# Batch norm and last layer of a graph network: PSUM operands, two GpSimd buffers, another division into parts, and h one stage ahead

## The chip, the core and the metric

The kernel runs on one core of a Trainium2 chip. The metric is the device time of one execution in microseconds. These engines and queues matter: TensorE (PE, with its weight loads as PEld), VectorE (DVE), ScalarE (ACT), GpSimd (POOL), and the DMA queue that SyncE (SP) issues. [...]

## The reference, cut to what matters

There are 128 graphs of 128 nodes and 64 features, and four layers, each of which adds to `x`. The change touches the end of layer 2 (a batch norm over all graphs) and layer 3.

```python
# layer 2: y has been computed and scaled to unit rows
m = mask[..., None]; cnt = jnp.sum(mask)
mean = jnp.sum(y * m, axis=(0, 1)) / cnt
var = jnp.sum((y - mean) ** 2 * m, axis=(0, 1)) / cnt
y = ((y - mean) / jnp.sqrt(var + BN_EPS) * gamma + beta) * m
x = x + jax.nn.relu(y)
# layer 3
h = jnp.maximum(_layernorm(x, axis=-1), 0.0)
messages = jnp.einsum('bij,bjh->bih', adjacency, h)
node_in = jnp.concatenate([h, messages], axis=-1)
x = x + jnp.tanh(node_in @ W1 + b1) @ W2 + b2
```

The mean and variance of layer 2 need every graph, so nothing of layer 3 can begin before layer 2's `y` of the last graph is known.

## The kernel before, in words

The work is tiled into 32 groups of 4 graphs; a tile of a group is 128 nodes by 4x64 values, all in float32. Layers 0, 1 and 2 of the groups run in one long pipeline that takes most of the span. `layer2_norm` (line 645) of a group leaves `y` in SBUF (`ys[g]`), and `add_sums` (line 670) adds its weighted sum to `ysum` in PSUM by TensorE. When the last group has come through, lines 771 to 776 have subtracted a shift from every `y`, squared it on ScalarE and added it to `ysq`. `total` (line 675) picks the wanted blocks of such a sum with VectorE (`own`) and adds them up with products by ones. Lines 779 to 789 make from both totals the two rows of the batch norm, `factor` and `summand` (together `affine_all`).

Then the end begins. The 32 groups are divided into parts (`PARTS`, line 52). For each group of a part `normed` (line 803) does these steps:

- L806 and L807 multiply by the factor and add the summand, in place in `ys[g]`. VectorE does this for the first part, GpSimd for all others.
- L808 multiplies by the node mask, which lies in PSUM (`nm_ps`), on VectorE.
- L809 takes the maximum with 0 and adds it to `x`, on VectorE.
- L811 takes the statistics of layer 3's layer norm, one instruction for each of the 4 graphs, on VectorE.

After the last group of a part `roots` (line 813) turns the part's statistics into `rstd3` and `less3`, with five or six small steps of VectorE, a square root on ScalarE (L823) and a reciprocal (L824). [...] between this square root and layer 3's tanh it loads a table (`ACT_TABLE_LOAD`).

Layer 3 of a group has three stages. `layer3_gather` (line 831) loads the transposed adjacency by DMA, computes `h`, multiplies `h` by the identity and by the adjacency on TensorE (16 products into `ps_hm`) and copies the result to SBUF on ScalarE (`hm`, L848). For groups below `LATE` (18) `h` is made by four activations on ScalarE (L841); from 18 on by two steps of VectorE (L836 and L307), and GpSimd adds the last bias to `x` (L838). `layer3_tanh` multiplies by W1 and takes the tanh on ScalarE (L855). `layer3_end` multiplies by W2, adds to `x` on VectorE (L863, `o`) and stores the result by DMA. The loop at lines 875 to 888 calls, for each group g of a part, a share of `normed` for the next part, then gather of g, tanh of g-1 and end of g-2.

That is the order in which the program states its steps. Within it a scheduler of the language may move a step forward on its engine where its inputs are there, so the engines' own orders differ somewhat: VectorE was up to ten groups ahead with `normed`. The language also sets all semaphores, from which steps read and write which tiles.

[...] Three pairs of banks are the tiles `blks`; the last pair, `fixed`, holds `nm_ps` at the end, and the other four banks with two more go round as `end_bank`.

Of the kernel before, what the change touches and what calls it, by code (L numbers as in the profile page):

```python
# [9 lines left out]
F32 = mybir.dt.float32  # L10
# [4 lines left out]
ALU = mybir.AluOpType  # L15
# [3 lines left out]
P = 128  # L19
F = 64  # L20
G = 4
NP = G // 2
H0 = 192
LN_EPS = 1e-5
BN_EPS = 1e-5

# [20 lines left out]
FIRST, FIRST_R = 0, ORDER.index((None, FULL))  # L47
N_PREPARE, N_AFTER = 14, 26
PACE, LAG = 0.85, 2.5
LATE = 18  # L50
LASTS = 1.9
PARTS = [2, 4, 6, 6, 6, 8]
AHEAD = 3
NBLK = 3
W = NP * H0
# [18 lines left out]
def network(ctx, tc, io, out, over=None, x1=None):  # L74
# [203 lines left out]
    def over_f(ap):  # L278

        return ap.unsqueeze(2).to_broadcast([P, G, F])  # L280

    def over_g(ap):

        return ap.unsqueeze(1).to_broadcast([P, G, F])

    def bank(name):
        return ps.tile([P, 512], F32, tag="ps", name=name)

    def flat(t):
        return t.rearrange("p a n -> p (a n)")  # L290
# [354 lines left out]
    def layer2_norm(g):  # L645
        xt, adjT, y = xs[g], adjTs[g], ys[g]
        h = yield from layernorm_relu(xt)
        zT = gathered(h, adjT, "zT")
        yield
        py = biased("L2_gnn_bias", F)  # L650
        project_pairs(py, zT, wbn, F)
        pyf = py[:, 0 : G * F]
        yf = y.rearrange("p b f -> p (b f)")
        nc.scalar.copy(yf, pyf)
        sq = work.tile([P, G, F], F32, tag="sq", name="sqy")
        nc.scalar.activation(sq.rearrange("p b f -> p (b f)"), pyf, AF.Square)
# [18 lines left out]
    def total(sums, name):  # L675
# [3 lines left out]
        pt = bank(name)  # L679
        for b in range(G):  # L680
            matmul(pt[:, 0:F], ones[0:G, :], own[:, b, :], start=b == 0, stop=b == G - 1)
        return pt[:, 0:F]


    rcnt = keep.tile([P, 2], F32, name="rcnt")
# [74 lines left out]


    spare = iter(range(10 ** 6))
    fixed = blks[NBLK - 1]

    def end_bank(name):

# [15 lines left out]
    nc.vector.scalar_tensor_tensor(moved[:, 0, :], total(ysum, "ps_row"), rcnt[:, 0:1], shift, ALU.mult, ALU.subtract)  # L782
    nc.vector.tensor_tensor(moved[:, 1, :], moved[:, 0, :], moved[:, 0, :], ALU.mult)
    nc.vector.scalar_tensor_tensor(factor, total(ysq, "ps_sq"), rcnt[:, 0:1], moved[:, 1, :], ALU.mult, ALU.subtract)
# [10 lines left out]
    rstd3 = keep.tile([P, NG, G], F32, name="rstd3")  # L795
    less3 = keep.tile([P, NG, G], F32, name="less3")
    NS = 6

    def part_stats(gs):
        t = work.tile([P, G, F], F32, tag="sqv", name="stats")  # L800
        return flat(t)[:, 0 : len(gs) * G * NS].rearrange("p (g b s) -> p g b s", b=G, s=NS)

    def normed(g, stats, engine):

        xt, y = xs[g], ys[g]
        engine.tensor_tensor(y, y, over_g(affine_all[:, 0, :]), ALU.mult)  # L806
        engine.tensor_tensor(y, y, over_g(affine_all[:, 1, :]), ALU.add)  # L807
        nc.vector.tensor_tensor(y, y, over_f(nm_ps[:, g * G : (g + 1) * G]), ALU.mult)  # L808
        nc.vector.scalar_tensor_tensor(xt, y, 0.0, xt, ALU.max, ALU.add)  # L809
        for b in range(G):  # L810
            nc.vector.bn_stats(stats[:, b, :], xt[:, b, :])  # L811

    def roots(gs, stats):
        r, less = rstd3[:, gs[0] : gs[-1] + 1, :], less3[:, gs[0] : gs[-1] + 1, :]
# [5 lines left out]
        nc.vector.tensor_tensor(r, s0, s1, ALU.add)  # L820
        late = gs[0] >= LATE
        nc.vector.tensor_tensor(less if late else s1, stats[:, :, :, 1], stats[:, :, :, 4], ALU.add)
        nc.scalar.activation(r, r, AF.Sqrt, bias=eps, scale=1.0 / F)  # L823
        nc.vector.reciprocal(r, r)  # L824
        if not late:
            nc.vector.scalar_tensor_tensor(less, s1, -0.5, r, ALU.mult, ALU.mult)


    hms, tTs = {}, {}

    def layer3_gather(g):
        adjT = adjp.tile([P, G, P], F32, tag="adjT", name="adjT")
        nc.sync.dma_start(flat(adjT), saved[g])
        h = work.tile([P, G, F], F32, tag="h", name="h")
        if g >= LATE:
            nc.vector.scalar_tensor_tensor(ys[g], over_f(less3[:, g, :]), -0.5, xs[g], ALU.mult, ALU.add)  # L836
            relu_scaled(ys[g], rstd3[:, g, :], h=h)
# [30 lines left out]
        parts.append(range(at, at + n))  # L868
        at += n
    assert at == NG  # L870
    stats = part_stats(parts[0])
    for g in parts[0]:
        normed(g, stats[:, g], nc.vector)
    roots(parts[0], stats)
    for gs, nxt in zip(parts, parts[1:] + [[]]):

        stats, done = part_stats(nxt) if nxt else None, 0
# [11 lines left out]
    layer3_tanh(NG - 1)  # L889
    layer3_end(NG - 2)  # L890
    layer3_end(NG - 1)

    if over is None:
        return
# [155 lines left out]
```

## Time and profile before

| what | us |
|---|---|
| median of 3 runs | 1395.79 |
| lowest and highest | 1392.44, 1399.84 |
| the profiled execution | 1398.05 |
| its span in the profile | 1396.2 |
| last group's sums begin on TensorE | 1268.81 |
| first `h` begins | 1287.08 |
| last square root of `roots` | 1355.57 |
| last gather begins | 1384.69 |
| GpSimd's last L807 ends | 1321.0 |

Times within the span count from its start. Over the whole span TensorE is busy 88%, VectorE 84%, ScalarE 71% and GpSimd 19% of the time. A row of a group of instructions gives the line, the engine, the operation, what it writes and reads, the shapes, how many there were, their busy time and mean length in ns, and the engine's idle time before them. Because a later instruction may start while the one before it ends, the distance between two starts can be less than a length. A helper's line stands for all of its callers: every product has line 103, so products are told apart by the tiles.

### The profile page before, as it was taken

Reading aid. Unit: us, or ns where it says so; the run is one execution under the profiler, and the core shown is the slowest. Engines: PE = TensorE matmul, PEld = TensorE weight load, DVE = VectorE, ACT = ScalarE, POOL = GpSimd, SP = SyncE. Lnnn points to the kernel's source line nnn. Section 1 sums busy time; section 2 is a strip of 40 time slices with the busy share of each in tenths; the row PEclk is TensorE's granted clock in tenths of the full one; section 3 lists DMA queues with packets and bytes.
Section 4 is the critical chain, followed back from the end, with each engine's and each line's share of the span. In section 5 each row is a group of like instructions: output and inputs, shape, how many; then the busy total and the mean of one; then the engine's idle time right before and its main releaser. Section 6 shows DMA issues by size and latency. Waiting matters only on the chain.

```text
span 1396.2 us, 29319 instructions
## 1 busy us (share of the span) xinstructions
PE 1232.2 (88%) x10964; PEld 959.3 (69%) x10964; DVE 1167.8 (84%) x2629; ACT 990.8 (71%) x1883; POOL 270.6 (19%) x322
## 2 busy tenths in 40 slices
PE   3788999999999999999999999999999999995787
PEld 1467777777777777777777777776777777763566
DVE  6898888888888888888888888888898888866973
ACT  1677777777777777777777777777777777753783
POOL 3111111111111111111111111111111111015830
PEclk9899999999999999999999999999999999997889
DMA  5443222322323222222222222223222212200345
GB/s 120 131 120 98 67 66 78 83 83 84 83 76 83 84 75 75 76 63 75 66 78 84 83 84 83 75 83 84 76 75 79 62 59 60 76 9 15 93 112 126
DMA packets 108788, 110.97 MB, mean 79 GB/s; under 512 B 42895, under 2 KB 88220, under 8 KB 108636
## 3 DMA queue, kind: packets, MB, share of 16 engines
q1 hardware_dynamic: 108636, 109.00, 28.5%
q8 instruction: 89, 1.46, 0.5%
q14 instruction: 63, 0.52, 0.1%
HBM read 52.70 MB, written 35.29 MB: 63 GB/s over the span
## 4 chain that ended last, share of the span: by engine, by line
PE 65%; ACT 17%; DVE 13%; issue 2%; SPq 1%; DMA 1%; DVEq 0%; POOL 0%; ACTq 0%; POOLq 0%
PE blk L103 24%; PE ps_pr L103 10%; ACT blk L560 9%; DVE acc L583 6%; PE ps_ag L103 5%; PE ps_p L103 5%; PE ps_sA L103 5%; PE ps_o L103 3%; PE ps_sB L103 3%; PE ps_q L103 2%; PE ps_ah L103 2%; PE ps_hm L103 2%; ACT q L465 2%; DVE leftT L424 1%; PE ps_key L103 1%
## 5 line engine op out<-in xcount | busy, mean ns | idle before, releaser
L583 DVE SCALAR_TENSOR_TENSOR acc<-blk,acc 128x768 f32<-128x768 f32 x576 | 543.1, 950 | 65.0 <-PE blk L103 38.9
L560 ACT COPY blk<-psort 128x768 f32<-128x768 f32 x544 | 436.1, 806 | 134.1 <-DVE acc L583 132.2
L103 PE MATMUL blk<-q,oh 128*128 128x192 bf16 x3072 | 318.2, 246 | 34.5 <-ACT blk L560 34.3
L103 PEld LDWEIGHTS <-oh 128*128 128x128 bf16 x3072 | 259.1, 98 | 89.3 <-issue 84.3
L103 PE MATMUL blk<-near_q,ohn 128*128 128x192 bf16 x1536 | 199.7, 246 | 22.4 <-ACT blk L560 22.1
L103 PEld LDWEIGHTS <-ohn 128*128 128x128 bf16 x1536 | 134.7, 98 | 59.9 <-issue 45.3
L468 POOL TENSOR_TENSOR q<-rest,q 128x768 bf16<-128x768 f32 x32 | 52.8, 1648 | 209.1 <-ACT q L467 209.1
L642 POOL TENSOR_TENSOR adjT<-adjT,ident 128x512 f32<-128x512 f32 x32 | 41.9, 1310 | 254.8 <-PE ps_ag L103 254.8
L668 POOL TENSOR_TENSOR y<-y,nrm 128x256 f32<-128x256 f32 x32 | 19.7, 615 | 363.7 <-PE blk L103 238.1
L634 ACT COPY msg<-ps_pr 128x512 f32<-128x512 f32 x64 | 37.5, 586 | 68.9 <-PE ps_pr L103 67.5
L541 DVE TENSOR_SCALAR ohn<-near_n 128x1536 bf16<-128x1536 bf16 x128 | 84.3, 695 | 0.0
L103 PE MATMUL ps_pr<-g,dT 128*128 128x128 f32 x512 | 78.8, 288 | 0.8 <-ACT dT L626 0.8
L560 ACT COPY blk<-psort_r 128x768 f32<-128x768 f32 x96 | 77.5, 807 | 0.5 <-DVE acc L583 0.4
L103 PEld LDWEIGHTS ps_pr<-g,dT 128*128 128x128 f32 x512 | 64.3, 191 | 11.5 <-issue 7.2
L103 PE MATMUL ps_ag<-adjT,msg 128*128 128x128 f32 x512 | 71.5, 283 | 0.6 <-ACT msg L634 0.5
L103 PEld LDWEIGHTS <-ones_b 3*128 3x128 bf16 (+2 forms) x280 | 26.0, 93 | 59.1 <-issue 51.5
L103 PEld LDWEIGHTS ps_ag<-adjT,msg 128*128 128x128 f32 x512 | 62.1, 191 | 5.9 <-ACT msg L634 5.5
L103 PE MATMUL ps_p<-wp,hs 128*128 128x384 f32 x128 | 59.0, 543 | 0.0
L626 ACT ACTIVATE dT<-ps_ag 128x512 f32<-128x512 f32 x96 | 56.8, 592 | 3.0 <-PE ps_ag L103 2.8
L103 PE MATMUL ps_q<-wq,hT 128*128 128x384 f32 x128 | 52.5, 534 | 4.4 <-ACT hT L328 0.8
L103 PE MATMUL ps_hm<-ident,h 128*64 128x128 f32 x248 | 43.6, 308 | 14.0 <-ACT h L841 13.9
L103 PE MATMUL ps_sA<-fro,acc 128*128 128x128 f32 x256 | 53.3, 290 | 2.1 <-ACT dT L626 1.9
(220 smaller groups left out, 2544.8 us busy)
## 6 DMA issues: line engine op xcount, KB each, us to landing
q_dram<-q SPq DMA_DIRECT2D x32, 567.0 KB
near_q<-q_dram SPq DMA_DIRECT2D x96, 189.0 KB
near_n<-n_dram SPq DMA_DIRECT2D x96, 126.0 KB
a<-in_adj_dram SPq DMA_DIRECT2D x32, 256.0 KB
adjT_dram<-adjT SPq DMA_DIRECT2D x32, 256.0 KB
adjT<-adjT_dram SPq DMA_DIRECT2D x32, 256.0 KB
psort_r<-psort SPq DMA_DIRECT2D x32, 228.0 KB
fro_r<-fro SPq DMA_DIRECT2D x32, 152.0 KB
```

Source lines behind the costliest of these rows:

```text
L103: return nc.tensor.matmul(o, w, x, **kw)
L424: nc.vector.scalar_tensor_tensor(flat(leftT), pk, float(NEAR), flat(mT), ALU.is_gt, ALU.mult)
L465: nc.scalar.copy(parts_q[:, 0, p, :], pq[:, 0:W])
L468: nc.gpsimd.tensor_tensor(parts_q[:, 2], rest, parts_q[:, 1], ALU.subtract)
L541: nc.vector.tensor_scalar(oh.rearrange("p t b n -> p (t b n)"), near_n[g % 2].rearrange("p t b n -> p (t b n)"), float(i + 1), None, ALU.i ...
L560: nc.scalar.copy(columns(t), psorts[g][in_segments(n)])
L583: nc.vector.scalar_tensor_tensor(acc, o, 0.0, acc, ALU.max, ALU.add)
L626: nc.scalar.activation(flat(dT), pa, AF.Relu)
L634: nc.scalar.copy(flat(msg), pm)
L642: nc.gpsimd.tensor_tensor(adjT, adjT, ident.unsqueeze(1).to_broadcast([P, G, P]), ALU.add)
L668: nc.gpsimd.tensor_tensor(y, y, over_f(nrm), ALU.mult)
```

## The change

Six things change, all in the end.

1. The sums of the last group no longer go through `ysum` and `ysq`. `total` takes the sums of the other 31 groups, and adds the last group's rows with four products whose weights are a broadcast column. The results lie in the two banks of `fixed`. The scaling of the last `y` moves from GpSimd to VectorE.
2. The first part has one group, and there are seven parts in place of six; `LATE` goes from 18 to 14.
3. L808 writes its result to PSUM (`y_ps`), and L809 reads it there. `y_ps` lies beside the mask in one bank of `fixed`.
4. The statistics of late parts, `rstd` and `less`, lie in PSUM too (`late_ps`), behind `y_ps`, in the same bank and the first columns of the next.
5. GpSimd writes its two steps to one of two buffers of an SBUF pool in turn instead of `ys[g]`, and reads the factor and summand from a copy (`affine_g`) that VectorE makes after the first part's `roots`.
6. `layer3_gather` is divided: `layer3_h` (the load of the adjacency, and `h`, with L836, L307 and L838 of late groups) is called for group g, and then gather of g-1, tanh of g-2 and end of g-3.

```diff
-LATE = 18
+LATE = 14
-PARTS = [2, 4, 6, 6, 6, 8]
+PARTS = [1, 3, 4, 6, 6, 6, 6]
...
-        add_sums(ysum, counted, y)
-        nc.gpsimd.tensor_tensor(y, y, over_f(nrm), ALU.mult)
+        if g < NG - 1:
+            add_sums(ysum, counted, y)
+            nc.gpsimd.tensor_tensor(y, y, over_f(nrm), ALU.mult)
+        else:
+            ends.append(total(ysum, "ps_row", pt=fixed[:, 0:512], more=(counted, y)))
+            nc.vector.tensor_tensor(y, y, over_f(nrm), ALU.mult)
...
-            matmul(pt[:, 0:F], ones[0:G, :], own[:, b, :], start=b == 0, stop=b == G - 1)
+            matmul(pt[:, 0:F], ones[0:G, :], own[:, b, :], start=b == 0, stop=b == G - 1 and more is None)
+        if more is not None:
+            weights, t = more
+            for b in range(G):
+                matmul(pt[:, 0:F], weights[:, b : b + 1].to_broadcast([P, P]), t[:, b, :], start=False, stop=b == G - 1)
...
-        add_sums(ysq, nm[:, g * G : (g + 1) * G], sq)
+        if g < NG - 1:
+            add_sums(ysq, nm[:, g * G : (g + 1) * G], sq)
+        else:
+            ends.append(total(ysq, "ps_sq", pt=fixed[:, 512:1024], more=(nm[:, g * G : (g + 1) * G], sq)))
...
-    nc.scalar.copy(fixed[:, 0:P], nm)
-    nm_ps = fixed[:, 0:P]
+    sizes = [P, G * F, 2 * (NG - LATE) * G]
+    nm_ps, y_ps, late_ps = (fixed[:, sum(sizes[:i]) : sum(sizes[: i + 1])] for i in range(len(sizes)))
...
+    nc.scalar.copy(nm_ps, nm)
...
+    def scales(g):
+        return (rstd3[:, g:], less3[:, g:]) if g < LATE else (late_ps[:, 0, g - LATE :], late_ps[:, 1, g - LATE :])
...
-        engine.tensor_tensor(y, y, over_g(affine_all[:, 0, :]), ALU.mult)
-        engine.tensor_tensor(y, y, over_g(affine_all[:, 1, :]), ALU.add)
-        nc.vector.tensor_tensor(y, y, over_f(nm_ps[:, g * G : (g + 1) * G]), ALU.mult)
-        nc.vector.scalar_tensor_tensor(xt, y, 0.0, xt, ALU.max, ALU.add)
+        affine = affine_all
+        if engine is nc.gpsimd:
+            affine, y = affine_g, flat(edge.tile([P, NP, W], F32, tag="acc0", name="y2"))[:, 0 : G * F].rearrange("p (b f) -> p b f", f=F)
+        engine.tensor_tensor(y, ys[g], over_g(affine[:, 0, :]), ALU.mult)
+        engine.tensor_tensor(y, y, over_g(affine[:, 1, :]), ALU.add)
+        nc.vector.tensor_tensor(y_ps, y, over_f(nm_ps[:, g * G : (g + 1) * G]), ALU.mult)
+        nc.vector.scalar_tensor_tensor(xt, y_ps, 0.0, xt, ALU.max, ALU.add)
...
-    def layer3_gather(g):
+    def layer3_h(g):
...
+        hs3[g] = h, adjT
+
+    def layer3_gather(g):
+        h, adjT = hs3.pop(g)
...
+    affine_g = keep.tile([P, 2, F], F32, name="affine_g")
+    nc.vector.tensor_copy(affine_g, affine_all)
...
         for k, g in enumerate(gs):
+            layer3_h(g)
             while done < min(len(nxt), math.ceil(len(nxt) * (k + 1) / max(1, len(gs) - 1))):
...
-            layer3_gather(g)
-            if g >= 1:
-                layer3_tanh(g - 1)
-            if g >= 2:
-                layer3_end(g - 2)
+            for back, stage in enumerate((layer3_gather, layer3_tanh, layer3_end), 1):
+                if g >= back:
+                    stage(g - back)
```

More of the change, by code (lines that the diff above doesn't have):

```diff
@@ L25 @@
 BN_EPS = 1e-5
+NS = 6
 THIRD = 42
@@ L673, in add_sums, with total @@
             matmul(sums[:, p, :], weights, t[:, 2 * p : 2 * p + 2, :].rearrange("p b f -> p (b f)"), start=False, stop=True, skip_group_check=True)
-    def total(sums, name):
+    def total(sums, name, pt=None, more=None):
         own = work.tile([G, G, F], F32, tag="own", name="own")
         nc.vector.tensor_tensor(own.rearrange("p (a b) f -> p a b f", a=NP), sums.rearrange("p a (b f) -> p a b f", f=F), ident[0:G, 0:G].rearrange("p (a b) -> p a b", a=NP).unsqueeze(3).to_broadcast([G, NP, 2, F]), ALU.mult)
-        pt = bank(name)
+        pt = bank(name) if pt is None else pt
         for b in range(G):
-            matmul(pt[:, 0:F], ones[0:G, :], own[:, b, :], start=b == 0, stop=b == G - 1)
+            matmul(pt[:, 0:F], ones[0:G, :], own[:, b, :], start=b == 0, stop=b == G - 1 and more is None)
[3 more added lines that the diff above has]
+                matmul(pt[:, 0:F], weights[:, b : b + 1].to_broadcast([P, P]), t[:, b, :], start=False, stop=b == G - 1)
         return pt[:, 0:F]
+    fixed = blks[NBLK - 1]
+    ends = []
     rcnt = keep.tile([P, 2], F32, name="rcnt")
@@ L762, in network @@
     spare = iter(range(10 ** 6))
-    fixed = blks[NBLK - 1]
     def end_bank(name):
@@ L781, in network @@
     moved = keep.tile([P, 2, F], F32, name="moved")
-    nc.vector.scalar_tensor_tensor(moved[:, 0, :], total(ysum, "ps_row"), rcnt[:, 0:1], shift, ALU.mult, ALU.subtract)
+    nc.vector.scalar_tensor_tensor(moved[:, 0, :], ends[0], rcnt[:, 0:1], shift, ALU.mult, ALU.subtract)
     nc.vector.tensor_tensor(moved[:, 1, :], moved[:, 0, :], moved[:, 0, :], ALU.mult)
-    nc.vector.scalar_tensor_tensor(factor, total(ysq, "ps_sq"), rcnt[:, 0:1], moved[:, 1, :], ALU.mult, ALU.subtract)
+    nc.vector.scalar_tensor_tensor(factor, ends[1], rcnt[:, 0:1], moved[:, 1, :], ALU.mult, ALU.subtract)
     nc.scalar.activation(factor, factor, AF.Sqrt, bias=eps_bn)
@@ L789, in network, with part_stats @@
     nc.vector.tensor_tensor(summand, beta_all, moved[:, 0, :], ALU.subtract)
-    nc.scalar.copy(fixed[:, 0:P], nm)
-    nm_ps = fixed[:, 0:P]
[L795 to L799, printed above, removed]
+    sizes = [P, G * F, 2 * (NG - LATE) * G]
+    nm_ps, y_ps, late_ps = (fixed[:, sum(sizes[:i]) : sum(sizes[: i + 1])] for i in range(len(sizes)))
+    y_ps = y_ps.rearrange("p (b f) -> p b f", f=F)
+    late_ps = late_ps.rearrange("p (a g b) -> p a g b", a=2, b=G)
+    nc.scalar.copy(nm_ps, nm)
+    rstd3 = keep.tile([P, LATE, G], F32, name="rstd3")
+    less3 = keep.tile([P, LATE, G], F32, name="less3")
+    def scales(g):
+        return (rstd3[:, g:], less3[:, g:]) if g < LATE else (late_ps[:, 0, g - LATE :], late_ps[:, 1, g - LATE :])
+    def part_stats(k):
         t = work.tile([P, G, F], F32, tag="sqv", name="stats")
-        return flat(t)[:, 0 : len(gs) * G * NS].rearrange("p (g b s) -> p g b s", b=G, s=NS)
+        return flat(t)[:, 0 : PARTS[k] * G * NS].rearrange("p (g b s) -> p g b s", b=G, s=NS)
     def normed(g, stats, engine):
         xt, y = xs[g], ys[g]
[L806 to L809, printed above, removed]
+        affine = affine_all
[5 more added lines that the diff above has]
+        nc.vector.scalar_tensor_tensor(xt, y_ps, 0.0, xt, ALU.max, ALU.add)
         for b in range(G):
@@ L813, in roots @@
     def roots(gs, stats):
-        r, less = rstd3[:, gs[0] : gs[-1] + 1, :], less3[:, gs[0] : gs[-1] + 1, :]
+        r, less = (t[:, 0 : len(gs), :] for t in scales(gs[0]))
         s0 = work.tile([P, NG // 4, G], F32, tag="mean", name="s0")[:, 0 : len(gs), :]
@@ L826, in roots @@
             nc.vector.scalar_tensor_tensor(less, s1, -0.5, r, ALU.mult, ALU.mult)
-    hms, tTs = {}, {}
-    def layer3_gather(g):
+    hs3, hms, tTs = {}, {}, {}
+    def layer3_h(g):
         adjT = adjp.tile([P, G, P], F32, tag="adjT", name="adjT")
@@ L835, in layer3_gather @@
         if g >= LATE:
-            nc.vector.scalar_tensor_tensor(ys[g], over_f(less3[:, g, :]), -0.5, xs[g], ALU.mult, ALU.add)
-            relu_scaled(ys[g], rstd3[:, g, :], h=h)
+            r, less = (t[:, 0, :] for t in scales(g))
+            nc.vector.scalar_tensor_tensor(ys[g], over_f(less), -0.5, xs[g], ALU.mult, ALU.add)
+            relu_scaled(ys[g], r, h=h)
             nc.gpsimd.tensor_tensor(xs[g], xs[g], over_g(b3o_all), ALU.add)
@@ L870, in network @@
     assert at == NG
-    stats = part_stats(parts[0])
+    stats = part_stats(0)
     for g in parts[0]:
@@ L874, in network @@
     roots(parts[0], stats)
-    for gs, nxt in zip(parts, parts[1:] + [[]]):
-        stats, done = part_stats(nxt) if nxt else None, 0
+    affine_g = keep.tile([P, 2, F], F32, name="affine_g")
+    nc.vector.tensor_copy(affine_g, affine_all)
+    for at, (gs, nxt) in enumerate(zip(parts, parts[1:] + [[]])):
+        stats, done = part_stats(at + 1) if nxt else None, 0
         for k, g in enumerate(gs):
+            layer3_h(g)
             while done < min(len(nxt), math.ceil(len(nxt) * (k + 1) / max(1, len(gs) - 1))):
@@ L883, in network @@
                     roots(nxt, stats)
-            layer3_gather(g)
-            if g >= 1:
-                layer3_tanh(g - 1)
-            if g >= 2:
-                layer3_end(g - 2)
-    layer3_tanh(NG - 1)
-    layer3_end(NG - 2)
-    layer3_end(NG - 1)
+            for back, stage in enumerate((layer3_gather, layer3_tanh, layer3_end), 1):
+                if g >= back:
+                    stage(g - back)
+    for g in range(NG, NG + 3):
+        for back, stage in enumerate((layer3_gather, layer3_tanh, layer3_end), 1):
+            if g - back < NG:
+                stage(g - back)
     if over is None:
```

## The prediction

> **What bounds the kernel now.** I read the page first (time by slice, chain of waits), then only the end of the span, since every changed line runs after 1268 us. Busy time by stage, in columns for TensorE, its weight load, VectorE, ScalarE, GpSimd, then the granted clock:
>
> ```profile
> core 0: us, PE busy (x) PEld busy (x) DVE busy (x) ACT busy (x) POOL busy (x), PEclk, DMA share, GB/s
> 1268.00:1275.00 7.00, 4.41 (x32) 3.03 (x29) 3.15 (x11) 0.91 (x4) 0.61 (x1) 0.86 0.00 1
> 1275.00:1287.00 12.00, 0.00 (x0) 0.00 (x0) 11.97 (x34) 0.30 (x1) 11.75 (x16) 0.50 0.00 0
> 1287.00:1296.40 9.40, 5.62 (x49) 4.91 (x49) 9.40 (x34) 5.88 (x13) 9.40 (x14) 0.65 0.23 58
> 1296.40:1324.30 27.90, 22.94 (x219) 17.34 (x219) 25.68 (x99) 20.95 (x50) 24.63 (x33) 0.88 0.38 94
> 1324.30:1344.90 20.60, 17.62 (x174) 13.64 (x170) 15.64 (x76) 17.10 (x40) 2.41 (x3) 0.83 0.43 109
> 1344.90:1357.40 12.50, 10.42 (x89) 7.90 (x84) 9.82 (x34) 10.46 (x19) 9.79 (x10) 0.73 0.35 97
> 1357.40:1384.70 27.30, 27.30 (x358) 23.10 (x354) 10.29 (x24) 13.61 (x28) 1.47 (x2) 1.00 0.68 166
> ```
>
> For 12 us VectorE and GpSimd are full and TensorE has nothing. To 1324 VectorE stays full; then ScalarE is the fullest beside TensorE; only from 1357.4 is TensorE without a gap, at 2.10 us a group (13 groups in 27.3 us). The chain of waits names the 12 us:
>
> ```profile
> 1275.43 0.86 DVE y L806
> ...
> 1277.84 1.73 DVE y L807 x2
> ...
> 1280.23 1.75 DVE x L809 x2
> ...
> 1286.83 0.22 DVE less L826
> ```
>
> All VectorE. The groups by line, while GpSimd runs (1287 to 1320) and later (1321 to 1348); the figure before the last bar is the mean in ns:
>
> ```profile
> L809 DVE SCALAR_TENSOR_TENSOR x<-y,x 128x256 f32<-128x256 f32 x16 | 10.9, 680 | 0.0
> L808 DVE TENSOR_TENSOR y<-y,blk 128x256 f32<-128x256 f32 x15 | 6.1, 405 | 0.0
> ```
>
> and after GpSimd's end:
>
> ```profile
> L809 DVE SCALAR_TENSOR_TENSOR x<-y,x 128x256 f32<-128x256 f32 x13 | 5.3, 410 | 0.0
> ```
>
> L809, both operands in SBUF, takes 680 ns beside GpSimd and 410 alone. L808, one operand in PSUM, takes 405 either way. So the trace shows the price that the change goes for. Last, the timeline around the square root of groups 18 to 23, VectorE's row and then ScalarE's:
>
> ```profile
> 1329.75 0.17 DVE L820 TENSOR_TENSOR rstd<-s,s 128x24 f32<-128x24 f32 x1
> ...
> 1344.89 1.28 ACT L823 ACT_TABLE_LOAD   x1
> 1346.19 0.31 ACT L823 ACTIVATE rstd<-rstd,eps 128x24 f32<-128x24 f32 x1
> 1346.99 1.28 ACT L855 ACT_TABLE_LOAD   x1
> ```
>
> Its input is ready at 1329.9; ScalarE comes to it at 1346.2, 16 us later, between two table loads. Today nobody minds.
>
> **Part by part**, in the profile's own time.
>
> *Sums of the last group.* Now, after `counted`: product 0.61, GpSimd's L668 0.62, L773 0.43, square 0.43, product 0.61, `own` 0.42, ones product 1.33, done at 1273.64. After: the first product becomes four of 128x64 (row of gout<-dT: 1.10 for its 8 passes), the scaling goes to VectorE (0.42, as L773), and the second product is again four, 1.10 to 1.33, with no `own` and no ones product behind it (those for the earlier groups lie beside the square). From 1268.81, with the gaps seen: 1.10+0.47+0.45+0.53+1.25 ends at 1272.6. Gain 1.0: the factor stands at 1274.2 instead of 1275.2. The copy of the mask to PSUM (0.27, at 1231 now) must wait for the first sum's reader; it lies beside that chain, else 0.27.
>
> *First part of one group, GpSimd held back.* GpSimd reads a copy of the factors, made after the first part, so group 0 runs alone: four dependent steps at 0.45, 0.5 for L788 and L789, statistics 0.6, small steps 0.8, root, reciprocal and product 0.75: 4.4 us, h(0) at 1278.6 (now 1287.1). This cannot all be kept. GpSimd starts near 1277 instead of 1275.2 and needs 0.78+0.82=1.6 a group: 4.8 for groups 1 to 3, to 1281.8. VectorE is 1.2 behind, and its roots cost what part 1's do now, 1291.98 to 1296.41, 4.4 us, because they stay in SBUF beside GpSimd. So h(1) starts near 1287.4 and h(2) near 1288.9, against 1296.4: 7.5 gained there.
>
> *y in PSUM.* L809 loses 0.27 in each of the 16 groups of that window, 4.3 us of VectorE. [...] the rows say 405 with and 410 without PSUM, so nothing. I take the row. No row has VectorE writing a 128x256 result to PSUM: [...] I take 0, since L808's reading shows none. There is one `y_ps`: each L808 waits for the L809 before it. Pitch between independent steps is 0.33, a dependent one 0.45: 0.12 a group, 3.7 in all, hidden wherever ScalarE is the limit.
>
> *Two buffers for GpSimd.* It may no longer run ahead to 1321 but is two groups ahead at most. VectorE's 1.3 a group plus 0.33 for `o` against GpSimd's 1.6: neither holds the other for long. Queued behind a waiting L808 are `o` and roots; behind a waiting L806, later L838.
>
> *h one stage ahead.* Now h(g) and hm(g) stand next to each other on ScalarE, with TensorE's gather between. From h(2) at 1296.41 to the end of h(13) at 1339.7 are 43.3 us: 12 groups of 1.50+0.59+0.47 are 30.7, four table loads with two roots 5.8; the remaining 6.8 is mostly ScalarE waiting for TensorE. With h ahead I leave a third, 2.3 (bounds 0 and 6.8). The load of adjT on SP moves with h, ahead of the stores of one more group; it needs the buffer of group g-4, whose gather is long issued, so four buffers hide it; without them one load would show per group.
>
> *Groups 14 to 17 late.* ScalarE loses 4x1.5=6.0; VectorE gains 8 steps of 0.33, GpSimd four L838 of 0.73 to 1.0; four bias products of 0.28 go.
>
> *Sum.* From h(1) at 1287.4 to the end of h(13): 13x1.50, 12x0.59, 11x0.47 are 31.8; tanh's first load and two root switches 7.1; waiting 2.3: 1328.6 (now 1339.7). Gather(14) comes one stage later than h(17) to gather(18) do now (3.1+2.1): 1333.8. 17 groups of 2.10 lead to gather(31) at 1369.5. What is late next: the norms of groups 20 to 31 now fall beside late groups. For six norms and five groups VectorE needs 6x1.3+5x0.99+0.9 to 3.0, 13.7 to 15.8, where TensorE needs 10.5. One such part fits in while ScalarE still works off h(11) to h(13); the other costs about 4 (bounds 0 and 10), and two root switches of 2.9, against ScalarE's 1.04 of slack a group, about 1. Gather(31) at 1374.5 instead of 1384.7: **10.2 us less**. The 11.5 behind it stays. The profiled run took 1398.05 with a span of 1396.2; the median is 1395.79. I take the gain from the median: 1385.5.
>
> **Rivals.**
> *B, ScalarE keeps its gaps.* Its 43.3 us are seldom VectorE's fault, so faster norms free little. All 6.8 of waiting stays (+4.5), and both late parts are in excess of TensorE (+4): 1394, a gain of about 2. For it: ScalarE's 17.1 of 20.6 after GpSimd is done. Against it: the first 12 us go in any case.
>
> *C, the root holds VectorE; slower.* From group 14 on, `rstd` and `less` lie in the bank of `y_ps` and the mask. [...] No row before has ScalarE and VectorE in such an order. [...] every L808 and L809 of the next part waits for the root, and behind L808 in VectorE's queue stand `o`, L836 and h. By the row that root ran 16 us after its input. There are three such roots; the first lies where VectorE is ahead (I count 0 of it). If the other two cost 10 each, the time is 1385.5+20, about 1406. It decides from 5 us each on. Against it: ScalarE has slack in the late stage (13.6 busy of 27.3), so its turn comes soon. Bounds of one wait: 0.3 and 16; I take the 1 above, as the 16 is from a full ScalarE.
>
> That PSUM does not help at all is the least likely: L808 and L863 (417) are the same engine, operands and neighbour.
>
> **How the numbers follow.** Forecast 0.66, own range 1377 to 1392 (waiting 0 or 6.8, late excess 0 or 10); B 0.16; C 0.18. A measurement here tells about 0.5%, 7 us, from no change: faster is below 1388.8, slower above 1402.8. The forecast gives 0.55 faster and 0.11 same; B 0.05 and 0.11; C 0.01, 0.01 and 0.16 slower: 0.61, 0.23, 0.16 in all. The range reaches from 1376 to 1401, leaving out most of C and some of the forecast's best.
>
> **What would show it.** Right: L809 near 0.41 while GpSimd runs; h(0) near 1278, h(2) near 1289; end of h(13) near 1329; TensorE without gaps from about 1334. Wrong, for B: hm still waiting for ps_hm before group 14. For C: VectorE idle, released by L823. Wrong otherwise: VectorE waiting for GpSimd at L808, or L838 holding GpSimd.

## The result, and the profile after

The changed kernel takes 1392.91 us in the median (1388.48 to 1396.45), the kernel before 1396.16 (1392.44 to 1401.05), measured in turn. The ratio is 0.9964, with a 95% interval of 0.9952 to 0.9976: it is faster by 3 to 7 us. The ratio itself stands for 5.0 us, just under half of the 10.2 us of the forecast; the two medians are 3.25 us apart. The profiled execution has a span of 1390.3 us (before: 1396.2).

Lines of the program have moved: L806 to L809 are now L834 to L837, the steps of `roots` L845 to L854 (square root L851, reciprocal L852), the late `h` L865 and L308, the copy `hm` L881, `o` L896, and products L104.

The busy time by stage in the changed kernel, in the columns of before (TensorE, weight load, VectorE, ScalarE, GpSimd, clock):

```profile
core 0: us, PE busy (x) PEld busy (x) DVE busy (x) ACT busy (x) POOL busy (x), PEclk, DMA share, GB/s
...
1275.00:1287.00 12.00, 2.74 (x24) 2.26 (x24) 10.57 (x48) 2.83 (x8) 7.88 (x12) 0.50 0.04 11
1287.00:1296.40 9.40, 7.54 (x54) 5.65 (x52) 7.76 (x37) 7.58 (x18) 6.44 (x9) 0.50 0.20 57
...
1344.90:1357.40 12.50, 8.35 (x96) 7.33 (x96) 9.06 (x34) 4.97 (x9) 7.69 (x11) 0.86 0.37 96
1357.40:1384.70 27.30, 22.37 (x276) 18.60 (x273) 15.64 (x54) 13.01 (x24) 7.38 (x11) 1.00 0.45 114
```

The first half went as meant: TensorE now has work from 1283.6 on, and VectorE and GpSimd are no longer full. The second half did not: from 1344.9 to 1357.4 TensorE is busy for 8.35 us where it was busy for 10.42, with no other engine full. It waits.

The groups of VectorE while GpSimd runs (1277 to 1316), the figure before the last bar being the mean in ns:

```profile
L836 DVE TENSOR_TENSOR blk<-y,blk 128x256 f32<-128x256 f32 x20 | 8.2, 410 | 0.7 <-POOL y L835 0.7
L837 DVE SCALAR_TENSOR_TENSOR x<-blk,x 128x256 f32<-128x256 f32 x19 | 7.9, 418 | 0.4
```

The step that took 680 ns beside GpSimd takes 418, and L836, which now writes its result to PSUM, takes 410 as before (405).

Now the place where the time goes: the timeline around the first and the second square root of late groups, a choice of rows:

```profile
1318.83 0.21 DVE L850 TENSOR_TENSOR blk<-stats 128x24 f32<-128x24 f32 x1
...
1322.48 0.42 DVE L896 TENSOR_TENSOR o<-x,blk 128x256 f32<-128x256 f32 x1 [2.04 <-PE blk L104]
1323.72 1.28 ACT L851 ACT_TABLE_LOAD   x1
...
1325.02 0.26 ACT L851 ACTIVATE blk<-blk,eps 128x24 f32<-128x24 f32 x1
...
1325.31 0.32 DVE L852 RECIPROCAL blk<-blk 128x24 f32<-128x24 f32 x1
...
1326.71 0.43 DVE L836 TENSOR_TENSOR blk<-y,blk 128x256 f32<-128x256 f32 x1
...
1344.18 0.21 DVE L850 TENSOR_TENSOR blk<-stats 128x24 f32<-128x24 f32 x1
...
1345.73 0.26 ACT L851 ACTIVATE blk<-blk,eps 128x24 f32<-128x24 f32 x1
...
1346.56 0.41 DVE L865 SCALAR_TENSOR_TENSOR y<-blk,x 128x256 f32<-128x256 f32 x1
...
1347.01 0.42 DVE L308 SCALAR_TENSOR_TENSOR h<-y,blk 128x256 f32<-128x256 f32 x1
...
1347.57 0.29 PE L104 MATMUL ps_hm<-ident,h 128*64 128x128 f32 x1 [1.75 <-DVE h L308]
...
1350.24 1.28 ACT L888 ACT_TABLE_LOAD   x1
...
1352.06 0.87 PE L104 MATMUL blk<-hm,w 128*64 128x128 f32 x5 [2.06 <-ACT tT L888]
```

Read it from the top. VectorE has finished its half of the root of groups 14 to 19 at 1319.04. ScalarE, busy for 5.5 of the next 6 us, most of all with `h` of early groups, comes to the square root 6 us later. In between VectorE does three `o` and nothing else; the next norm (L836, of group 20) starts at 1326.71, 7.7 us after the root was handed over, though GpSimd's part of it was done at 1318.0. The norms of groups 20 to 25 then run about one to a late group, so their root, the second, comes only at 1345.73. There `h` of group 19, whose own factors were ready since 1325, stands behind that root on VectorE; TensorE waits 1.75 us for it, and another 2.06 for a tanh whose table is loaded first. The third root (1366.1) repeats the first of these waits with group 25.

### The profile page after: what moved, and what is told of

The parts are those of the page before. It is cut to its first block, busy times and chain, and to the rows that moved or that the text cites. A ratio compares the mean times of both kernels' runs of the same rounds, so it can differ in the third digit from the quotient of the medians.

```text
span 1390.3 us, 29353 instructions
## 1 busy us (share of the span) xinstructions
PE 1230.0 (88%) x10968; PEld 959.8 (69%) x10968; DVE 1162.0 (84%) x2643; ACT 986.6 (71%) x1870; POOL 267.7 (19%) x327
## 4 chain that ended last, share of the span: by engine, by line
PE 64%; ACT 18%; DVE 12%; issue 2%; SPq 1%; DMA 1%; POOL 0%; DVEq 0%; ACTq 0%
PE blk L104 24%; PE ps_pr L104 10%; ACT blk L561 9%; DVE acc L584 6%; PE ps_ag L104 5%; PE ps_p L104 5%; PE ps_sA L104 5%; PE ps_o L104 3%; PE ps_sB L104 3%; PE ps_q L104 2%; PE ps_ah L104 2%; ACT q L466 2%; PE ps_hm L104 2%; DVE leftT L425 1%; PE ps_key L104 1%
## 5 line engine op out<-in xcount | busy, mean ns | idle before, releaser
L584 DVE SCALAR_TENSOR_TENSOR acc<-blk,acc 128x768 f32<-128x768 f32 x576 | 543.1, 949 | 66.3 <-PE blk L104 40.7
L104 PE MATMUL blk<-q,oh 128*128 128x192 bf16 x3072 | 319.5, 247 | 33.6 <-ACT blk L561 33.5
L104 PEld LDWEIGHTS <-oh 128*128 128x128 bf16 x3072 | 259.9, 99 | 88.4 <-issue 83.2
L104 PE MATMUL blk<-near_q,ohn 128*128 128x192 bf16 x1536 | 201.1, 247 | 22.4 <-ACT blk L561 22.1
L104 PEld LDWEIGHTS <-ohn 128*128 128x128 bf16 x1536 | 135.6, 98 | 60.2 <-issue 45.7
L104 PE MATMUL ps_pr<-g,dT 128*128 128x128 f32 x512 | 78.8, 288 | 0.8 <-ACT dT L627 0.8
L104 PEld LDWEIGHTS ps_pr<-g,dT 128*128 128x128 f32 x512 | 64.3, 191 | 11.5 <-issue 7.2
L104 PE MATMUL ps_ag<-adjT,msg 128*128 128x128 f32 x512 | 71.5, 283 | 0.6 <-ACT msg L635 0.4
L104 PEld LDWEIGHTS ps_ag<-adjT,msg 128*128 128x128 f32 x512 | 62.1, 191 | 6.0 <-ACT msg L635 5.4
L104 PEld LDWEIGHTS <-ones_b 3*128 3x128 bf16 (+2 forms) x276 | 25.6, 93 | 58.7 <-issue 51.2
L104 PE MATMUL ps_p<-wp,hs 128*128 128x384 f32 x128 | 58.3, 537 | 0.0
L104 PE MATMUL ps_q<-wq,hT 128*128 128x384 f32 x128 | 51.9, 528 | 4.4 <-ACT hT L329 0.8
L104 PE MATMUL ps_sA<-fro,acc 128*128 128x128 f32 x256 | 53.3, 290 | 2.1 <-ACT dT L627 2.1
L104 PE MATMUL ps_sA<-fro_r,acc 128*128 128x128 f32 x256 | 49.7, 276 | 0.0
```

Source lines behind the costliest of these rows:

```text
L584: nc.vector.scalar_tensor_tensor(acc, o, 0.0, acc, ALU.max, ALU.add)
```

## The experiments

The theory: from group 14 on, the factors lie in one tile of PSUM with `y_ps`, and the language keeps the accesses to that tile in order. So a norm that writes `y_ps` may not pass a root that writes its factors there, and the norms and `h` behind it wait for ScalarE. In the expectations of e1 to e3 this is theory 1, but stated of the bank, as in rival C of the prediction; it was e2 that turned "bank" into "tile". The rivals: the order goes by bank (then another bank cures it); it is only `h` that stands behind the root; or VectorE is simply too full among late groups (theory 2 of the expectations; then no cure helps).

All measurements in one table. A is the time from the end of `counted` to the factor, B from the factor to the end of the last `o`, C from the start of the copy `hm` of group 14 to that of group 31, all three from one profiled execution of each, in us. C would be 35.7 at the pace of 2.10 a group that TensorE kept before from 1357.4 to 1384.7 (17 groups). A, B and C are of single executions, and differ for reasons other than the edit too: `counted`, which comes ahead of everything changed, ends between 1266.9 and 1272.0 in these 15 profiles.

| kernel | median us | ratio, 95% interval | A | B | C |
|---|---|---|---|---|---|
| before | | 1 | 6.42 | 114.9 | 42.5 |
| the change | 1392.91 | 0.9964, 0.9952 to 0.9976 | 7.09 | 107.9 | 47.8 |
| e1, late factors in SBUF | 1385.00 | 0.9912, 0.9895 to 0.9930 | 6.72 | 99.1 | 38.7 |
| e2, late factors in the other bank | 1392.48 | 0.9968, 0.9953 to 0.9982 | 6.73 | 109.3 | 49.2 |
| e3, root behind the last `h` | 1384.45 | 0.9906, 0.9893 to 0.9920 | 7.22 | 101.3 | 43.9 |
| e4, before with the new sums | 1397.45 (one run) | | 6.72 | 116.0 | 42.5 |
| e5, e1 and e3 | 1384.00 | 0.9906, 0.9891 to 0.9922 | 7.45 | 97.0 | 40.0 |
| e6, e1 and second sum in its own tile | 1385.13 (one run) | | 6.74 | 99.7 | 38.1 |
| e7, `h` not ahead | 1397.99 | 0.9996, 0.9981 to 1.0011 | 7.28 | 112.7 | 49.8 |
| e8, `y` in SBUF | 1397.07 | 0.9990, 0.9978 to 1.0002 | 6.71 | 109.7 | 45.4 |
| e9, parts of before | 1390.97 | 0.9938, 0.9922 to 0.9955 | 6.73 | 106.2 | 46.5 |
| e10, GpSimd in place | 1415.69 | 1.0137, 1.0105 to 1.0170 | 6.72 | 133.1 | 49.2 |
| e11, e5 with the old sums | 1380.53 | 0.9870, 0.9854 to 0.9886 | 6.21 | 97.4 | 40.0 |
| e12, before with `y` in PSUM | 1418.79 | 1.0166, 1.0137 to 1.0194 | 7.07 | 136.1 | 42.7 |
| e13, e11 with parts of before | 1385.44 | 0.9919, 0.9906 to 0.9933 | 6.20 | 101.0 | 41.4 |

### e1: the late factors in SBUF

```diff
-    rstd3 = keep.tile([P, LATE, G], F32, name="rstd3")
-    less3 = keep.tile([P, LATE, G], F32, name="less3")
+    rstd3 = keep.tile([P, NG, G], F32, name="rstd3")
+    less3 = keep.tile([P, NG, G], F32, name="less3")
...
-        return (rstd3[:, g:], less3[:, g:]) if g < LATE else (late_ps[:, 0, g - LATE :], late_ps[:, 1, g - LATE :])
+        return rstd3[:, g:], less3[:, g:]
```

> The changed kernel with rstd and less of the late groups in SBUF, as before; all else kept. Theory 1 (the bank order: the square root on ScalarE lies in the bank of y_ps and of the late factors, so VectorE's norms of the next part and h of the part's last group stand behind it): h of group 19 runs ahead of the root of groups 20 to 25, the gap in TensorE near 1344 to 1348 goes, VectorE begins the norms of group 20 soon after 1319 instead of 1326.7, and the time is 5 to 9 us below the changed kernel (about 0.990 to 0.993 of the kernel before). Theory 2 (VectorE is simply late with the norms beside late groups): the gaps stay, L865 slows from 0.42 to 0.68 beside GpSimd, and the time is that of the changed kernel or 1 to 3 us more (0.996 to 0.999).

It takes 1385.00 us, ratio 0.9912 (0.9895 to 0.9930), some 7 us less than the changed kernel. The same root in its timeline:

```profile
1320.07 0.44 DVE L848 TENSOR_TENSOR rstd<-s,s 128x24 f32<-128x24 f32 x1
...
1321.62 0.41 DVE L836 TENSOR_TENSOR blk<-y,blk 128x256 f32<-128x256 f32 x1
...
1323.99 0.40 DVE L836 TENSOR_TENSOR blk<-y,blk 128x256 f32<-128x256 f32 x1
...
1325.43 0.32 ACT L851 ACTIVATE rstd<-rstd,eps 128x24 f32<-128x24 f32 x1
...
1326.42 0.40 DVE L836 TENSOR_TENSOR blk<-y,blk 128x256 f32<-128x256 f32 x1
```

ScalarE is still 4.9 us late with the root, but the next part's norms go on ahead of it. The second late root comes some 10 us earlier, counted from the factor, and C falls from 47.8 to 38.7. So VectorE was not too full. It even had slower steps here: with the factors in SBUF, `h` (L308) beside GpSimd took up to 0.77 us instead of 0.42.

The clock of TensorE could be another cause. In the changed kernel the granted clock was 0.50 from 1352.1 to 1355.5, inside C, and in e1 it was 1.00 in all of C. By an estimate from these figures, half speed for 3.4 us costs TensorE at most 1.7 us of work, out of the 9.1 by which C fell.

### e2: the late factors in the other bank of the same tile

```diff
-    nm_ps, y_ps, late_ps = (fixed[:, sum(sizes[:i]) : sum(sizes[: i + 1])] for i in range(len(sizes)))
+    nm_ps, y_ps, late_ps = (fixed[:, at : at + n] for at, n in zip((0, P, 512), sizes))
```

> The changed kernel with rstd and less of the late groups in the second bank of the pair, y_ps and the mask alone in the first. The root no longer shares a bank with L836 and L837, but still with L865 of earlier groups. Theory 1: the norms of group 20 begin near 1319, the next root is ready near 1335 instead of 1344, and 3 to 8 us go (0.991 to 0.994 of the kernel before). If it is only h of groups 19 and 25 that counts, the time stays within 2 us of the changed kernel. Theory 2: no change (0.996).

The ratio is 0.9968 (0.9953 to 0.9982): nothing changes, where theory 1, as then stated of the bank, had 3 to 8 us. The instructions of every engine and their order are the same as in the changed kernel. So it isn't the bank that orders root and norm, as rival C of the prediction had it. Theory 2 had named this number, but e1 excludes it. That the order goes by the tile as a whole fits e1 and e2. For the factors it isn't shown: a third kernel with them in a PSUM tile of their own, which would separate the tile from PSUM itself, was not tried. e6 below does this for another pair of steps.

### e3: the root behind the part's last `h`

```diff
             layer3_h(g)
+            if nxt and done == len(nxt):
+                roots(nxt, stats)
...
-                if done == len(nxt):
+                if done == len(nxt) and k == len(gs) - 1:
                     roots(nxt, stats)
```

> The changed kernel with the small steps and the root of a part stated one group later, behind h of the current part's last group (groups 7, 13, 19, 25), so that this h no longer stands behind the root in the bank; norms still do. Theory 1: h of 19 and 25 run ahead, each of the two gaps shrinks by 2 to 3 us, 3 to 5 us go in all (0.992 to 0.994 of the kernel before). Theory 2: the root comes a group later and the next part's h with it, 2 to 4 us more (0.998 to 0.999).

It takes 1384.45 us, ratio 0.9906 (0.9893 to 0.9920): 8 us less than the changed kernel, more than I expected. The factors still lie in PSUM, and the next norms still wait for the root; but `h` of groups 19 and 25 now goes ahead of the root, 2.8 and 2.6 us before the square root. Here is that of group 19:

```profile
1342.30 0.40 DVE L308 SCALAR_TENSOR_TENSOR h<-y,blk 128x256 f32<-128x256 f32 x1
...
1345.09 0.26 ACT L851 ACTIVATE blk<-blk,eps 128x24 f32<-128x24 f32 x1
```

C falls by 3.9 us of the 9.1 that e1 takes away; the held norms are still in it. The early stage is 1.9 us shorter too (from the factor to `hm` of group 13: 51.45 instead of 53.36): ScalarE now does its last early `h` ahead of this root and its two table loads.

### e5: both cures together

> Both cures together: late factors in SBUF and the root stated behind the last h of the part. Theory 1 (what cost time was h of groups 19 and 25, and the norms, standing behind the root in one tile): with the factors in SBUF nothing is left for the later root to free, so the time is that of the kernel with late factors in SBUF within 2 us (0.990 to 0.993 of the kernel before). Rival (the later root helps by itself, because the table loads then meet a better moment on ScalarE): a further 3 to 5 us (0.987 to 0.989).

1384.00 us, ratio 0.9906 (0.9891 to 0.9922). In the one profiled execution B is 2.1 us below e1, but the medians of e1, e3 and e5 lie within 1 us. So the two cures don't add up: each takes away what the other would have, steps of VectorE whose inputs are there standing behind a reciprocal that waits for ScalarE. A further gain of the later root by itself, the rival of this expectation, doesn't show.

### e4 and e6: the sums

> The kernel before with the last group's sums of the changed kernel alone. By the prediction's step the factor stands 5.4 us after the end of `counted` (before: 6.4). By the changed kernel's trace it is 7.1: the ones products and `own` of the second sum are on the path (1.1 and 0.4), and L797 and L798 come behind the second sum's products (0.6).

e4 is the kernel before with part 1 of the change alone. One run took 1397.45 us, within the scatter of before. A is 6.72 where it was 6.42; the forecast had 5.4, and the expectation, read from the changed kernel, 7.1. The timeline of the changed kernel shows what I had missed:

```profile
1271.55 0.41 DVE L684 TENSOR_TENSOR own<-blk,ident 4x256 f32<-4x256 f32 x1
...
1272.01 1.10 PE L104 MATMUL blk<-own,ones 4*128 4x64 f32 x8 [0.77 <-DVE own L684]
1273.04 1.47 PE L104 MATMUL blk<-sqv,nm 128*128 128x64 f32 x8
1274.55 0.28 DVE L797 SCALAR_TENSOR_TENSOR moved<-blk,rcnt,shift 128x64 f32<-128x64 f32 x1 [2.60 <-PE blk L104]
```

`own` of the earlier groups doesn't lie beside the square; it stands on VectorE behind the scaling and the shift, and its products by ones (1.10) push the last four products back. And L797, which needs only the first sum, complete at 1270.7, runs after the second one.

e6 gives the second sum a bank of its own, on top of e1:

```diff
-            ends.append(total(ysq, "ps_sq", pt=fixed[:, 512:1024], more=(nm[:, g * G : (g + 1) * G], sq)))
+            ends.append(total(ysq, "ps_sq", more=(nm[:, g * G : (g + 1) * G], sq)))
```

> Late factors in SBUF, and the second sum in a bank of its own tile instead of the second bank of the pair. If order is kept for the pair as one, L797 and L798 now run before the second sum's products end (0.6 less), and the factor stands 6.1 us after the end of `counted` instead of 6.7. If L797 waited for something else, it stays at 6.7.

L797 then runs 2.0 us before the last products, so it was the shared tile that had held it. It was not the bank, since both sums had a bank each before, and not PSUM, since the second sum is still in PSUM. A is nevertheless 6.74, because the last products took 1.63 us there instead of the 1.10 of e1 and e4. That goes with the clock and not with the tile: the granted clock (the third figure from the end) was 0.62 while they ran, and 1.00 in e1 and e4.

```profile
1274.54:1276.17 1.63, 1.63 (x9) 1.44 (x8) 0.00 (x0) 0.00 (x0) 0.00 (x0) 0.62 0.06 15
```

The clock falls to 0.50 close to this place (the mean from 1275 to 1287 is 0.50 before, in the changed kernel and in e10, and 0.57 in e9), sometimes before and sometimes behind the end of the last products, and A follows it: 7.09 in the changed kernel, where they took 1.47 at 0.70, and 6.72 in e4, where they took 1.10 at 1.00. Where the last products take 1.10, A is 6.20 with the old sums (e11, e13) and 6.71 to 6.73 with the new ones (e1, e2, e4, e8, e9, e10). So part 1 of the change loses 0.5 us. With 1.10 in place of 1.63, A of e6 would be 6.2 (an estimate from these rows): its own bank takes the loss back, near the 6.1 expected, but gains nothing over the old sums.

### e7 and e8: one part of the change undone

e7 calls `layer3_h` in the same stage as the gather:

```diff
-            layer3_h(g)
...
-            for back, stage in enumerate((layer3_gather, layer3_tanh, layer3_end), 1):
+            layer3_h(g)
+            for back, stage in enumerate((layer3_gather, layer3_tanh, layer3_end)):
```

> The changed kernel with h in the stage of its products again. By the prediction's step the ScalarE stage to the end of h(13) becomes 4.5 us longer, and in the late stage h of 19 and 25 stand behind the root as before: 1397 to 1398, no gain left (0.999 to 1.001). Rival: h one stage ahead is worth nothing while ScalarE is full, the time stays within 2 us of the changed kernel (0.995 to 0.998).

Ratio 0.9996 (0.9981 to 1.0011). The difference to the change, 0.0032, is 4.5 us; with both intervals, 2 to 7. In the profile, the stretch from the factor to `hm` of group 13 is 3.9 us longer than in the changed kernel, C 2.0.

e8 leaves `y` in SBUF:

```diff
-        nc.vector.tensor_tensor(y_ps, y, over_f(nm_ps[:, g * G : (g + 1) * G]), ALU.mult)
-        nc.vector.scalar_tensor_tensor(xt, y_ps, 0.0, xt, ALU.max, ALU.add)
+        nc.vector.tensor_tensor(y, y, over_f(nm_ps[:, g * G : (g + 1) * G]), ALU.mult)
+        nc.vector.scalar_tensor_tensor(xt, y, 0.0, xt, ALU.max, ALU.add)
```

> The changed kernel with y kept in SBUF: L836 writes GpSimd's buffer in place and L837 reads it there. L837 takes 0.68 beside GpSimd instead of 0.42. By the prediction's step some 16 of these lie where VectorE is the limit: 4 us more than the changed kernel (0.998 to 1.000). Rival: VectorE has slack in the ScalarE stage, and only the first part counts: 1 us more (0.996 to 0.998).

Ratio 0.9990 (0.9978 to 1.0002): with the two buffers beside it, `y` in PSUM is worth about 3.6 us; with both intervals, 1 to 6. The profiled execution (1391.81 us) is one of the fastest of the twelve, so the table's A, B and C show less. It came by another way than I expected. These are the groups from 1277 to 1316:

```profile
L837 DVE SCALAR_TENSOR_TENSOR x<-y,x 128x256 f32<-128x256 f32 x19 | 8.8, 470 | 0.0
L836 DVE TENSOR_TENSOR y<-y,blk 128x256 f32<-128x256 f32 x19 | 7.7, 411 | 4.1 <-POOL y L835 4.1
```

Both inputs of L837 lie in SBUF, but beside a GpSimd that often waits it takes 470 ns, not 680: 1.0 us in these 19 steps. The larger loss is that VectorE waits 4.1 us for GpSimd here, and 0.7 in the changed kernel. With `y` in SBUF the buffer comes free only behind L837; with `y` in PSUM it is free after L836.

### e9 and e13: the parts

```diff
-LATE = 14
+LATE = 18
-PARTS = [1, 3, 4, 6, 6, 6, 6]
+PARTS = [2, 4, 6, 6, 6, 8]
```

> The changed kernel with the parts of before (2, 4, 6, 6, 6, 8 groups) and 18 early groups instead of 14; everything else of the change stays. Theory 1 (the loss is the late root ordered with y_ps): only two roots lie in PSUM instead of three, but four more groups of h stand on ScalarE ahead of tanh and four more bias products; the first h comes about 2 us later. I expect 1391 to 1398, ratio 0.996 to 1.001. If the short first part is worth what I forecast (7.5 us at the start), it comes out at 1397 or more; if the parts matter little, within 2 us of the changed kernel (0.9964).

Ratio 0.9938 (0.9922 to 0.9955), below the changed kernel's and below the ratios that I expected (0.996 to 1.001). So in the changed kernel the new division doesn't pay. The likely reason is the third late root in PSUM that it brings. e13 makes the same edit where the late roots have been cured (e11):

> The version with late factors in SBUF, the root behind the part's last h and the sums of before (0.987), now with the parts of before (2, 4, 6, 6, 6, 8 groups, 18 early). The changed kernel with these parts came to 0.9938, below its own 0.9964, but there it also has two late roots in PSUM instead of three. If the short first part and the 14 early groups are worth the 7.5 us and 4 early h's that my forecast gave them, this comes to 0.991 to 0.993. If the parts matter little by themselves, 0.986 to 0.988, and the 0.9938 is from the one late root fewer. If the longer parts are better by themselves, below 0.985.

There the parts of before cost time: 0.9919 (0.9906 to 0.9933) against 0.9870. By the ratios that is 6.8 us, by B 3.6. So the new parts are worth something once the roots hold nobody.

### e10 and e12: GpSimd in place

e10 takes the two buffers out of the change (GpSimd works in `ys[g]`, as before, but still reads the copy of the factors):

```diff
-            affine, y = affine_g, flat(edge.tile([P, NP, W], F32, tag="acc0", name="y2"))[:, 0 : G * F].rearrange("p (b f) -> p b f", f=F)
+            affine = affine_g
```

> The changed kernel with GpSimd writing in place into its one buffer and reading the one table of factors, as before; GpSimd is not held back behind the first part. My forecast gave the two buffers themselves nothing ('neither holds the other for long'). If that holds, within 2 us of the changed kernel: ratio 0.995 to 0.998. If starting at once beside the first part costs the first h about 1 us and running further ahead gains it back, the same. Only if the two buffers carry weight of their own does it come to 0.999 or more, or below 0.994.

I had expected next to nothing. It is slower than before by 1.4% (ratio 1.0137, 1.0105 to 1.0170), 24 us more than the changed kernel. One small step of a root lasts 23.4 us, to 1316.78. GpSimd has run step upon step until 1316.74, and its next and last one begins at 1316.83. L837, which reads `y` in PSUM, is not slower beside this GpSimd (1277 to 1316):

```profile
L837 DVE SCALAR_TENSOR_TENSOR x<-blk,x 128x256 f32<-128x256 f32 x7 | 2.9, 418 | 0.1
```

e12 asks whether `y` in PSUM alone brings the long step:

```diff
+    y_ps = fixed[:, P : P + G * F].rearrange("p (b f) -> p b f", f=F)
...
-        nc.vector.tensor_tensor(y, y, over_f(nm_ps[:, g * G : (g + 1) * G]), ALU.mult)
-        nc.vector.scalar_tensor_tensor(xt, y, 0.0, xt, ALU.max, ALU.add)
+        nc.vector.tensor_tensor(y_ps, y, over_f(nm_ps[:, g * G : (g + 1) * G]), ALU.mult)
+        nc.vector.scalar_tensor_tensor(xt, y_ps, 0.0, xt, ALU.max, ALU.add)
```

> The kernel before with one edit alone: VectorE's product with the mask is written to PSUM and read there. In the run with GpSimd in place, one subtraction of the roots (128x16, all in SBUF) took 23.4 us and ended with GpSimd's last step. Theory S: once VectorE's long steps have an operand in PSUM, GpSimd, which waits for nobody, runs without a gap, and VectorE's next step with all operands in SBUF gets no turn until GpSimd is done. Then it happens here too: one small step of VectorE's between 1290 and 1300 lasts until GpSimd's end near 1318, and the time is 1408 to 1422, ratio 1.008 to 1.018. Rival: that stall belongs to the other parts of the change; then VectorE only gains the 0.27 us of 16 groups, and the time is 1391 to 1396, ratio 0.997 to 1.000.

It does: 1418.79 us, ratio 1.0166 (1.0137 to 1.0194). From its timeline, VectorE's rows and GpSimd's last:

```profile
1291.02 25.95 DVE L818 TENSOR_TENSOR s<-stats 128x16 f32<-128x16 f32 x1
...
1315.54 1.39 POOL L808 TENSOR_TENSOR y<-y,affine_all 128x256 f32<-128x256 f32 x2
...
1316.90 0.17 DVE L820 TENSOR_TENSOR s<-stats 128x16 f32<-128x16 f32 x1
```

In the kernel before the same step took 0.71 us:

```profile
L817 DVE TENSOR_TENSOR s<-stats 128x16 f32<-128x16 f32 x1 | 0.7, 707 | 0.0
```

Here it ends at 1316.97, 0.04 us after GpSimd's last one. ScalarE waits 22.9 us for the root, and TensorE is busy for 2.4 of these 26 us. So theory S holds in what it says of the order of events; that the step waits for access to SBUF is inferred from its operands and not shown.

### e11: the best version

e11 is e5 with the last group's sums as before.

> The changed kernel with the last group's sums as before, the late factors in SBUF and the root behind the part's last h. Theory: the new sums lose 0.3 to 0.7 us instead of gaining 1.0, so this comes out 0 to 1 us below the version with new sums: ratio 0.989 to 0.991, about 1383.5. If the new sums do gain 1 us by the clock of the whole run, it comes out at 0.9910 to 0.9920.

It takes 1380.53 us, ratio 0.9870 (0.9854 to 0.9886): 18 us less than before, and the fastest here. That is 0.0036, or 5 us, below e5, more than I expected. The profiles show 1.2 us of it in A, of which 0.7 is the clock (last products 1.84 us in e5, 1.10 here) and 0.5 the sums. Another 1.4 us lie ahead of `counted`; where the rest comes from stays open.

## Why the prediction was right in direction and wrong in size

**The failed step** is the term "What is late next": the late excess, about 4 for the norms and "about 1" for the two root switches. C was 47.8 us in the changed kernel, 12.1 above the 35.7 of TensorE alone, not 5. Group by group against a pace of 2.10, `hm` loses 6.1 us around the second root (groups 19 to 21; at most 1.7 of it by the clock, see e1), 3.1 around the third (25 to 29), and 2.8 elsewhere. What I had priced at 4 is VectorE's work, and that was about right: with the order taken away (e1), the excess is 3.0. What I had priced at 1 is the roots, and they cost 9.2. I had written the mechanism down, in rival C (an assumption there: no row of before showed it), and set its first case to 0 ("the first lies where VectorE is ahead"). But VectorE is no longer far ahead, because GpSimd may lead it by two groups only, and from 1319 to 1325 ScalarE was busy 93% of the time, more than beside the row with the 16 us wait (81%). The first root ran 6.2 us after its input and held the norm for 7.7. And I read C only as norms held back; that `h` of the part's last group stands behind the root too was in its list of what is queued, but not in its price. C's order came about, then, but not its outcome, slower than before. The second and third root ran only 1.6 and 1.9 us after their input, because ScalarE has slack there (4.97 us busy of 12.50 from 1344.9, 13.01 of 27.30 from 1357.4), as I had argued against C; their cost of 6.1 and 3.1 stayed under the 10 each of C's sum.

The other steps:

- **Sums: wrong.** 1.0 us gained was forecast; at equal clock 0.5 was lost (6.72 for 6.20), in the profiled run 0.67. The products by ones are on the path, and L797 and L798 wait for the shared tile.
- **Start: wrong for the first `h`, right for the next.** The first `h` came 6.4 us after the factor (forecast 4.4), since VectorE took the next group's norm ahead of group 0's small steps and waited 0.7 us for GpSimd there. The next `h`, which counts, came 12.4 us after it (forecast 13.2).
- **`y` in PSUM: the rate is right, the isolation wrong.** 418 ns, not 680, also beside a GpSimd without gaps (e10). It pays (e8) only together with the two buffers; alone it costs 23 us (e12). That e8's 3.6 us is near my 4.3 is in part luck: beside the two buffers the slow step would have been 470 ns, and most of the loss is waiting for GpSimd.
- **Two buffers: wrong.** I gave them nothing, as neither engine holds the other for long. That is so, but they are worth 24 us (e10). The reason, as far as the traces show it: with them GpSimd stops now and then (it waits 6.0 us for VectorE from 1278 to 1316), and no small step of VectorE takes over 0.6 us there.
- **`h` ahead: right.** 4.5 us forecast (6.8 less 2.3), 4.5 measured (e7; 2 to 7), so the exact match is luck. Rival B, whose 1394 is near the measured time, falls all the same: from `h` of group 2 to that of group 13 ScalarE idled 8.8 us before (my remainder of 6.8 was low, as its steps overlap) and 3.7 after, and the waits of `hm` for TensorE's `ps_hm` in it went from 5.1 to 1.0.
- **End of `h` of group 13: right.** Forecast 1328.6, profiled 1328.9. Partly luck: a later factor (1276.6 for 1274.2) was made good by a stretch 2.1 us shorter behind it.
- **TensorE without gaps from 1334: wrong.** It idled at 1346 and 1366, each time before an `h` of VectorE, and at 1350 before a tanh.

The sum closes. The last gather begins at 1379.3 instead of 1374.5. These 4.8 us are 0.8 for a later `counted`, which is scatter; 1.65 for the sums (7.09 for 5.4), of which 0.4 is the clock; minus 4.7 from the factor to gather 14 (which begins at 1331.5, 54.9 after the factor, instead of 59.6), because `h` of group 13 took 2.1 less and gather 14 followed it by 2.6 instead of 5.2; and 7.1 from there to gather 31 (47.8 instead of 40.7). Without these 4.7, which I had not foreseen, the sum would leave a gain of 0.7 us.

## What to carry to other kernels

Before small results are put into a free corner of a tile that another engine's loop writes, ask whose steps that tile puts in one order: here moving the same values to SBUF gained 7 us, though some steps got slower by it. A step that waits for a slow engine belongs behind the work that is ready, in program order too (8 us in e3). And judge parts of a change together: one that is worth 4 us beside its partner cost 23 alone.

## What the runs showed of the hardware that was not expected

In two runs a step of VectorE lasted for as long as GpSimd went on without a gap. In e12 a step with two inputs in SBUF lasted 26 us, in which GpSimd ran 39 steps of about 0.73 us, one beginning every 0.68. In e10 one lasted 23.4 us and ended as GpSimd first paused, for 0.1 us. In the kernel before, where GpSimd also ran without a gap from 1291 to 1317 (26.0 of 26.0 us busy), the step of e12 took 0.71 us. Why it took so long in e12 and e10 alone, and why the roots of the first parts passed there (0.2 to 0.8 us a step in e12), is not shown.

The clock granted to TensorE moved a measured step by as much as an edit did: the same eight passes of the last sum took 1.10 us at 1.00 (e4), 1.47 at 0.70 (the changed kernel) and 1.63 at 0.62 (e6).
